# Scan output taken from the state, skip scaled ahead of the merge, one convolution tap moved, six score tiles instead of seven

## The chip, the cores and the metric

The kernel runs on one core of a Trainium2 chip. The metric is the device time of one execution in microseconds (us). TensorE (PE) does matmuls and transposes, VectorE (DVE) and ScalarE (ACT) do elementwise work, GpSimd (POOL) a little of it, and SyncE (SP) issues nearly all DMAs. All data are fp32.

## The reference

The input is (4, 64, 64, 256). A first layer, a Mamba-like block, is followed by self-attention over the 4096 positions of each image. Cut to what matters:

```
xz = layernorm(x) @ in_proj_W ;  x_proj, z = split(xz)              # 384 channels each
windows = 2x2 windows of x_proj                                     # 4 tokens each
# for each direction (forward, and backward on flipped windows):
dt = silu(dt_raw @ dt_W + dt_b);  dA = exp(dt * a);  dBx = dt * B * x    # 8 states n
state = dA_t * state + dBx_t ;  y_t = sum_n state[n] * C_t[n] ;  y += x * D
y_ssm = 0.5 * (y_fwd + y_bwd)
y_conv = gelu(depthwise3x3(x_proj) @ pw_W)
y = alpha * y_ssm + (1 - alpha) * y_conv ;  x_out = x + (y * silu(z)) @ out_W
x1 = x_out + mlp(layernorm(x_out))
# attention, per image:
scores = (x1 Wg + bg)(x1 Wf + bf)^T ;  out = gamma * (softmax(scores) (x1 Wh + bh) Wo + bo) + x1
```

## The kernel before

The layer is cut into 32 blocks of 8 image rows (`at` = 0 to 31, 8 blocks an image); a block is 512 positions, and its four window tokens t = 0 to 3 are four groups of 128 windows on the partitions. Each block runs `scan(at)` and, beside it, the generators of `side(at)`: the convolution of the block before (`conv`, `depthwise`), its gate, its `tail` (pointwise matmul, output projection, MLP, and the attention's inputs, written to DRAM) and the `head` of the next. Every `yield` gives a cost by which `first_layer` interleaves them. The instructions are recorded in that order; a scheduler then sets the order in which they stand on each engine.

In the scan, `decays` computes on ScalarE `e = exp(dt * a_n)` for one state and direction (L392). `turned` transposes 128x128 pieces of e on TensorE into a PSUM bank (L449; three banks, and a fourth in image 0). Then VectorE does, for each step j = 3n + k (state n, k = 0 to 2) and each direction d:

- `decayed`: p = dA * h, where h is the state so far (L461), or, for the first step, dA * B * u (L457), with u = dt * x;
- `given`: y[t] += p * C (L467);
- `carried`: h = u * B + p for k < 2 (L476).

y thus takes only the decayed part p. The part of u that enters at token t itself is put in once for all states: `cb` = sum over n of B * C, and y[t] starts as u0 * cb (ScalarE, L424) plus u1 * cb (VectorE, L426), for all four tokens. The forward direction is one step ahead of the backward one. The order of a step is p forward, p backward, y forward, h forward, h backward, y backward.

`merge` turns y back to channels (L554), adds the skip x * (D_f + D_b) on VectorE (L555, `dsum`), then scales by alpha / 2 on ScalarE (L558, `half_a`). `depthwise` sums nine taps: in image 0 two of three channel groups are done on TensorE wholly, in the other images only the first group, and of it seven taps on TensorE (L567) and two on VectorE (L584, L588).

Attention of image b starts when its 8 blocks are done. Narrow queries (`attend`, 128 positions) go in 8 steps; after each, `next(beside)` moves the next query's `weights` on by one stage, and `fill(RATE)` adds 7.2 us worth of the layer. `weights` computes scores transposed in two groups g of four PSUM banks q0 to q3 (L836), which the layer's matmuls use too (`aside`); ScalarE copies each pair of banks to one tile e of the pool `ep` (tag "eq", L844), so a query has four tiles, and step k of `attend` (L1030) reads tile k // 2:

```
for k in range(NI):                    # NI = 8
    ...
    nc.tensor.matmul(acc[:, : DIM + 1], lhsT=es[k // 2][:, k % 2, a : a + P], rhs=vt[:, s, :], ...)
    next(own, None)
    next(beside, None)
    fill(RATE)
```

Maxima (L850, L852), the subtraction (L871) and the exponential (L872) follow. With `EBUF = 7` the pool has seven such tiles. When the layer is finished, the rest of the queries go by twos (`late_weights`, `attend_late`, L929, L937, L1008), in buffers of other pools.

Of the kernel before, what the change touches and what calls it, by code (L numbers as in the profile page):

```python
# [21 lines left out]
F32 = mybir.dt.float32  # L22
AF = mybir.ActivationFunctionType
ALU = mybir.AluOpType
# [4 lines left out]
P = 128  # L29
DIM = 256  # L30
INNER = 384
NST = 8
RANK = 48
KD = DIM // P
KI = INNER // P
KF = 2 * DIM // P
VBUF = 5
EBUF = 7
ROWS = 8
TOK = 512  # L40
CK = DIM // 8
# [18 lines left out]
def block_then_attention_kernel(  # L60
# [18 lines left out]
    nc = tc.nc  # L79
# [26 lines left out]
    wp = ctx.enter_context(tc.tile_pool(name="w", bufs=1))  # L106
# [26 lines left out]
    vp = ctx.enter_context(tc.tile_pool(name="vp", bufs=VBUF))  # L133
    ep = ctx.enter_context(tc.tile_pool(name="ep", bufs=EBUF))
    ps = ctx.enter_context(tc.tile_pool(name="ps", bufs=3, space=PSUM))
# [8 lines left out]
    def bank():  # L144
        return ps.tile([P, TOK], F32, tag="ps", name="bank")
# [50 lines left out]
    dsum = wp.tile([P, KI], F32, name="dsum")  # L196
# [2 lines left out]
    nc.scalar.activation(alpha, v("gate", 0, KI), AF.Sigmoid)  # L199
    half_a = wp.tile([P, KI], F32, name="half_a")  # L200
    nc.vector.tensor_scalar(half_a, alpha, 0.5, None, ALU.mult)
    one_a = wp.tile([P, KI], F32, name="one_a")
    nc.vector.tensor_scalar(one_a, alpha, -1.0, 1.0, ALU.mult, ALU.add)
    b_fg = wp.tile([P, 1], F32, name="b_fg")
# [182 lines left out]
    def decays(at, n, d):  # L387
        _, _, dts, es = steps[at]
        e = three.tile([P, KI, 3 * P], F32, tag="e", name="e")
        lo = P * (1 - d)  # L390
        for f in range(KI):
            nc.scalar.activation(  # L392
                e[:, f, :], dts[d][:, f, lo : lo + 3 * P], AF.Exp,
                scale=a_sc[:, d, f * NST + n : f * NST + n + 1],
            )
        es[d, n] = e
# [16 lines left out]
    def scan(at, ensue):  # L413

        bc, cb, dts, es = steps[at]
        if at == 0:
            yield from inputs(at, 0)
        yield from inputs(at, 1)
        decays(at, 0, 1)
        u = us[at, 0], us[at, 1]  # L420
        y = one.tile([P, 4, INNER], F32, tag="y", name="y")

        for t in range(4):
            nc.scalar.activation(y[:, t, :], u[0][:, t, :], AF.Copy, scale=cb[:, 2 * t : 2 * t + 1])  # L424
        for t in range(4):
            nc.vector.scalar_tensor_tensor(  # L426
                y[:, t, :], u[1][:, t, :], cb[:, 2 * t + 1 : 2 * t + 2], y[:, t, :], ALU.mult, ALU.add
            )
            if t % 2:
                yield 1.1  # L430

        order = ((0, 1, 2, 3), (3, 2, 1, 0))
        hs = {}

        def place(d, j):

            if at < NBLK and (2 * j + d) % 4 == 3:
                return pso.tile([P, TOK], F32, tag="pso", name="pa")  # L440
            return bank()

        def turned(d, j):

            n, k = divmod(j, 3)
            off = (order[d][k + 1] - (1 - d)) * P
            pa = place(d, j)
            for f in range(KI):
                nc.tensor.transpose(pa[:, f * P : (f + 1) * P], es[d, n][:, f, off : off + P], ident)  # L449
            return pa  # L450

        def decayed(d, j, pa):
            n, k = divmod(j, 3)
            t0 = order[d][k]
            p = three.tile([P, INNER], F32, tag="p", name="p")
            if k == 0:
                nc.vector.scalar_tensor_tensor(  # L457
                    p, pa[:, :INNER], bc[:, t0, d, n : n + 1], u[d][:, t0, :], ALU.mult, ALU.mult
                )
            else:  # L460
                nc.vector.tensor_tensor(p, pa[:, :INNER], hs[d], ALU.mult)  # L461
            return p

        def given(d, j, p):
            n, k = divmod(j, 3)
            t = order[d][k + 1]
            nc.vector.scalar_tensor_tensor(  # L467
                y[:, t, :], p, bc[:, t, d, NST + n : NST + n + 1], y[:, t, :], ALU.mult, ALU.add
            )

        def carried(d, j, p):
            n, k = divmod(j, 3)
            if k < 2:
                t = order[d][k + 1]
                hs[d] = three.tile([P, INNER], F32, tag="h", name="h")
                nc.vector.scalar_tensor_tensor(  # L476
                    hs[d], u[d][:, t, :], bc[:, t, d, n : n + 1], p, ALU.mult, ALU.add
                )

        early = True  # L480
        pas = {}
        if early:
            pas[0, 0] = turned(0, 0)
        for j in range(3 * NST + 1):
            n, k = divmod(j, 3)
            first, second = j < 3 * NST, j > 0
            if early and k == 2 and n + 1 < NST:
                decays(at, n + 1, 1)
            if not early and first and k == 0 and n > 0:
                decays(at, n, 1)  # L490
            if first and k == 1 and n + 1 < NST:
                decays(at, n + 1, 0)
            if not early:
                if first:
                    pas[0, j] = turned(0, j)
                if second:
                    pas[1, j - 1] = turned(1, j - 1)
            p0 = decayed(0, j, pas.pop((0, j))) if first else None
            p1 = decayed(1, j - 1, pas.pop((1, j - 1))) if second else None
            if first:  # L500
                given(0, j, p0)
                if early:
                    if j + 1 < 3 * NST:
                        pas[0, j + 1] = turned(0, j + 1)
                    pas[1, j] = turned(1, j)
                yield 1.3
                carried(0, j, p0)
            if second:
                carried(1, j - 1, p1)
                given(1, j - 1, p1)  # L510
            yield 2.0
            if j == 3 * NST - 4:
                ensue = ensue()
            if j >= 3 * NST - 4:
                for cost in ensue:
                    yield cost
                    if j < 3 * NST and cost > 2.0:
                        break
        merged[at] = y
# [27 lines left out]
    def merge(at):  # L547

        y = merged.pop(at)
        xc = heads[at][1]  # L550
        for f in range(KI):
            py = bank()
            for t in range(4):
                nc.tensor.transpose(py[:, t * P : (t + 1) * P], y[:, t, f * P : (f + 1) * P], ident)  # L554
            nc.vector.scalar_tensor_tensor(xc[:, f, :], xc[:, f, :], dsum[:, f : f + 1], py, ALU.mult, ALU.add)  # L555
            yield 1.1
        for f in range(KI):
            nc.scalar.activation(xc[:, f, :], xc[:, f, :], AF.Copy, scale=half_a[:, f : f + 1])  # L558

    def depthwise(ydw, dense, taps):  # L560

        for f in range(KI):
            if f < dense:
                pc = aside()
                for tap in range(taps):
                    dy, dx = divmod(tap, 3)
                    nc.tensor.matmul(  # L567
                        pc, lhsT=diags[9 * f + tap], rhs=xp[:, f, dy : dy + ROWS, dx : dx + W],
                        start=(tap == 0), stop=(tap == taps - 1),
                    )  # L570
                    if tap % 3 == 2:
                        yield 2.6
                if taps == 9:
                    nc.scalar.copy(ydw[:, f, :], pc)
                    continue
            o = ydw[:, f, :].rearrange("p (r c) -> p r c", r=ROWS)
            for tap in range(taps if f < dense else 0, 9):
                dy, dx = divmod(tap, 3)
                x_tap = xp[:, f, dy : dy + ROWS, dx : dx + W]
                w_tap = v("dw", 9 * f + tap)  # L580
                if tap == 0:
                    nc.vector.tensor_scalar(o, x_tap, w_tap, None, ALU.mult)
                elif f < dense and tap == taps:
                    nc.vector.scalar_tensor_tensor(  # L584
                        o, x_tap, w_tap, pc.rearrange("p (r c) -> p r c", r=ROWS), ALU.mult, ALU.add
                    )
                else:
                    nc.vector.scalar_tensor_tensor(o, x_tap, w_tap, o, ALU.mult, ALU.add)  # L588
                if tap % 3 == 2:
                    yield 2.0  # L590
# [3 lines left out]
    def conv(at):  # L594
        b = at // NBLK
        ydw = one.tile([P, KI, TOK], F32, tag="ff", name="ydw")
        ydws[at] = ydw
        yield from depthwise(ydw, KI - 1 if b == 0 else 1, 9 if b == 0 else 7)

    def next_head(at):  # L600

# [460 lines left out]
    while True:  # L1062
        b, q = divmod(a, NQ)
# [119 lines left out]
```

## Time and profile before

| | |
|---|---|
| median of three runs | 5304.44 us (5290.6 to 5309.06) |
| profiled execution, its time | 5294.06 us |
| its span | 5292.2 us |
| TensorE matmul / weight load, busy | 4958.2 us (94%) / 3545.8 us (67%) |
| VectorE busy | 4574.8 us (86%), 8433 instructions |
| ScalarE busy | 3573.8 us (68%), 5499 instructions |
| granted TensorE clock, mean | 0.981 |

"Busy" is the time in which at least one instruction of an engine runs. The end of a matmul is modelled, so TensorE's busy time is an upper value. A row of the groups by line gives the source line, engine, operation, tiles written and read, shapes and count, then the busy time and the mean ns of one instruction, then the idle time of the engine just ahead of it and what ended that. A line of the stretches gives, for each engine, its busy us and in brackets its instructions.

### The profile page before, as it was taken

The numbers are of one execution on the slowest core, as the hardware profiler recorded it, in microseconds if no ns is written. First come the engines' busy times: TensorE is split into PE (matmuls) and PEld (weight loads), VectorE is DVE, ScalarE is ACT, GpSimd is POOL, SyncE is SP. The second block draws the span as 40 slices with busy tenths as digits, with TensorE's granted clock in tenths as the row PEclk, the third lists the DMA queues.
The fourth block names the chain that finished last, engine by engine and source line by source line (L and its number), as shares of the span: only waits on it lengthen the run. The fifth ranks groups of instructions, "written<-read, shape, count | busy, mean of one in ns | idle before, by whom it ended". The sixth has DMA issues, their size and how long they took to land. (4 is left out here: it accounts for less than half of the span.)

```text
span 5292.2 us, 77188 instructions
## 1 busy us (share of the span) xinstructions
PE 4958.2 (94%) x27186; PEld 3545.8 (67%) x27186; DVE 4574.8 (86%) x8433; ACT 3573.8 (68%) x5499; POOL 205.4 (4%) x304
## 2 busy tenths in 40 slices
PE   7999999999999999999999999999999999999999
PEld 4555565667666666666666666666667667888887
DVE  7999999999899888999999999988999976666665
ACT  5777777677767766777767777776677745555554
POOL 0000000000000000000000000000000000000000
PEclk7999999999999999999999999999999999999999
DMA  1001010334333333343333333433343335555554
GB/s 48 26 32 31 19 38 20 106 118 119 100 117 113 111 112 112 117 121 116 100 117 112 117 117 113 121 107 113 100 122 118 115 116 152 148 147 147 147 148 138
DMA packets 330291, 554.20 MB, mean 105 GB/s; under 512 B 51504, under 2 KB 85936, under 8 KB 329904
## 3 DMA queue, kind: packets, MB, share of 16 engines
q1 hardware_dynamic: 327328, 547.30, 35.2%
q8 instruction: 215, 3.52, 0.3%
q10 hardware_dynamic: 2576, 1.97, 0.1%
q14 instruction: 172, 1.41, 0.1%
HBM read 490.28 MB, written 58.79 MB: 104 GB/s over the span
## 5 line engine op out<-in xcount | busy, mean ns | idle before, releaser
L1030 PE MATMUL acc<-vt,eq 128*128 128x257 f32 x4736 | 1207.0, 391 | 25.3 <-DVE res L978 12.3
L392 ACT ACTIVATE e<-dt,a_sc 128x384 f32<-128x384 f32 x1536 | 851.9, 611 | 357.0 <-PE bank L449 350.3
L1030 PEld LDWEIGHTS acc<-vt,eq 128*128 128x128 f32 x4736 | 874.0, 194 | 256.2 <-issue 121.1
L467 DVE SCALAR_TENSOR_TENSOR y<-p,bc,y 128x384 f32<-128x384 f32 x1536 | 938.0, 611 | 0.4
L449 PEld LDWEIGHTS bank<-ident,e 128*128 128x128 f32 x4320 | 522.5, 143 | 323.9 <-issue 123.5
L449 PE MATMUL bank<-ident,e 128*128 128x128 f32 x4320 | 648.8, 280 | 81.1 <-DVE p L461 38.6
L1008 PE MATMUL bank<-vt,eT 128*128 128x257 f32 x2560 | 645.8, 382 | 0.0
L476 DVE SCALAR_TENSOR_TENSOR h<-u,bc,p 128x384 f32<-128x384 f32 x1024 | 613.0, 614 | 0.2
L461 DVE TENSOR_TENSOR p<-bank,h 128x384 f32<-128x384 f32 x960 | 512.6, 547 | 52.0 <-PE bank L449 50.9
L1008 PEld LDWEIGHTS bank<-vt,eT 128*128 128x128 f32 x2560 | 478.6, 189 | 83.7 <-issue 13.9
L844 ACT COPY eq<-q 128x512 f32<-128x512 f32 x592 | 302.6, 592 | 133.9 <-PE q L836 131.1
L942 DVE TENSOR_TENSOR mx<-mx,eT 128x512 f32<-128x512 f32 x378 | 261.7, 692 | 148.3 <-ACT eT L937 117.0
L872 ACT ACTIVATE eq<-eq 128x1024 f32<-128x1024 f32 x296 | 308.6, 1053 | 103.1 <-DVE eq L871 101.2
L871 DVE TENSOR_TENSOR eq<-eq,nb 128x1024 f32<-128x1024 f32 x296 | 358.6, 1223 | 7.6 <-ACT nb L867 6.8
L937 ACT COPY eT<-q 128x512 f32<-128x512 f32 x432 | 221.4, 597 | 198.7 <-PE q L929 198.7
L392 ACT ACT_TABLE_LOAD x256 | 328.4, 1283 | 40.1 <-PE bank L449 36.3
L852 DVE TENSOR_TENSOR mx<-mx,eq 128x512 f32<-128x512 f32 x444 | 308.8, 696 | 38.7 <-ACT eq L844 30.7
L588 DVE SCALAR_TENSOR_TENSOR ydw<-xp,vec,ydw 128x512 f32<-128x512 f32 x472 | 338.4, 743 | 1.2
L457 DVE SCALAR_TENSOR_TENSOR p<-bank,bc,u 128x384 f32<-128x384 f32 x480 | 291.6, 607 | 23.3 <-PE bank L449 23.0
L619 PE MATMUL q<-ydw,wpw 128*128 128x512 f32 x576 | 272.1, 603 | 16.8 <-ACT eq L844 16.6
L967 DVE TENSOR_TENSOR eT<-eT,m 128x1024 f32<-128x1024 f32 x216 | 247.6, 1219 | 42.3 <-ACT m L964 42.3
L1008 PE MATMUL acc<-vt,eT 128*128 128x257 f32 x896 | 273.9, 388 | 0.0
(152 smaller groups left out, 7282.1 us busy)
## 6 DMA issues: line engine op xcount, KB each, us to landing
vt<-vod SPq DMA_DIRECT2D x1616, 257.0 KB, 2.8
vod<-vst SPq DMA_DIRECT2D x32, 514.0 KB, 4.0
xo<-in_x_dram SPq DMA_DIRECT2D x256, 64.0 KB, 2.6
xt<-in_x_dram SPq DMA_DIRECT2D x256, 64.0 KB, 1.9
x1d<-xo SPq DMA_DIRECT2D x32, 512.0 KB, 2.9
res<-x1d SPq DMA_DIRECT2D x74, 128.0 KB, 2.7
out_dram<-res SPq DMA_DIRECT2D x296, 32.0 KB, 1.6
fgd<-fg SPq DMA_DIRECT2D x32, 256.0 KB, 2.0
```

The source lines that it names most:

```text
L392: nc.scalar.activation(e[:, f, :], dts[d][:, f, lo : lo + 3 * P], AF.Exp, scale=a_sc[:, d, f * NST + n : f * NST + n + 1],)
L449: nc.tensor.transpose(pa[:, f * P : (f + 1) * P], es[d, n][:, f, off : off + P], ident)
L461: nc.vector.tensor_tensor(p, pa[:, :INNER], hs[d], ALU.mult)
L467: nc.vector.scalar_tensor_tensor(y[:, t, :], p, bc[:, t, d, NST + n : NST + n + 1], y[:, t, :], ALU.mult, ALU.add)
L476: nc.vector.scalar_tensor_tensor(hs[d], u[d][:, t, :], bc[:, t, d, n : n + 1], p, ALU.mult, ALU.add)
L588: nc.vector.scalar_tensor_tensor(o, x_tap, w_tap, o, ALU.mult, ALU.add)
L844: nc.scalar.copy(e[:, j, :], pr[2 * a + j])
L852: nc.vector.tensor_tensor(mx, mx, e[:, r % 2, :], ALU.max)
L871: nc.vector.tensor_tensor(e8, e8, nb.unsqueeze(1).broadcast_to([P, 8, P]), ALU.add)
L872: nc.scalar.activation(e, e, AF.Exp)
L1008: nc.tensor.matmul(sums[c][:, : DIM + 1], lhsT=e[:, r % 2, s, c * P : (c + 1) * P], rhs=vt[:, s, :], start=(n == 0 and s == 0), stop=(n == ...
L1030: nc.tensor.matmul(acc[:, : DIM + 1], lhsT=es[k // 2][:, k % 2, a : a + P], rhs=vt[:, s, :], start=(n == 0 and s == 0), stop=(n == 2 * NI ...
```

## The change

- `given` reads h where `carried` forms one (k < 2) and p elsewhere. y[1] and y[2] then need no start from cb: the forward direction's first contribution (n = 0) starts them as a ScalarE copy with scale C. Only y[0] and y[3] start from u and cb.
- The order of a step is p forward, p backward, h forward, h backward, y forward, y backward. A dead switch (`early`) goes.
- `merge` scales the skip first on ScalarE, by `half_d` = alpha / 2 * (D_f + D_b), a new constant; VectorE then adds alpha / 2 times the turned y.
- In images 1 to 3 six taps of the first channel group are on TensorE and three on VectorE.
- `EBUF` is 6.

```diff
-EBUF = 7
+EBUF = 6
...
+    half_d = wp.tile([P, KI], F32, name="half_d")
+    nc.vector.tensor_tensor(half_d, half_a, dsum, ALU.mult)
...
-        for t in range(4):
+        for t in (0, 3):
             nc.scalar.activation(y[:, t, :], u[0][:, t, :], AF.Copy, scale=cb[:, 2 * t : 2 * t + 1])
-        for t in range(4):
+        for t in (0, 3):
             nc.vector.scalar_tensor_tensor(
                 y[:, t, :], u[1][:, t, :], cb[:, 2 * t + 1 : 2 * t + 2], y[:, t, :], ALU.mult, ALU.add
             )
-            if t % 2:
-                yield 1.1
+        yield 1.1
...
         def given(d, j, p):
             n, k = divmod(j, 3)
             t = order[d][k + 1]
-            nc.vector.scalar_tensor_tensor(
-                y[:, t, :], p, bc[:, t, d, NST + n : NST + n + 1], y[:, t, :], ALU.mult, ALU.add
-            )
+            h = hs[d] if k < 2 else p
+            c = bc[:, t, d, NST + n : NST + n + 1]
+            if d == 0 and n == 0 and k < 2:
+                nc.scalar.activation(y[:, t, :], h, AF.Copy, scale=c)
+            else:
+                nc.vector.scalar_tensor_tensor(y[:, t, :], h, c, y[:, t, :], ALU.mult, ALU.add)
...
             if first:
-                given(0, j, p0)
-                if early:
-                    if j + 1 < 3 * NST:
-                        pas[0, j + 1] = turned(0, j + 1)
-                    pas[1, j] = turned(1, j)
+                carried(0, j, p0)
+                if j + 1 < 3 * NST:
+                    pas[0, j + 1] = turned(0, j + 1)
+                pas[1, j] = turned(1, j)
                 yield 1.3
-                carried(0, j, p0)
             if second:
                 carried(1, j - 1, p1)
+            if first:
+                given(0, j, p0)
+            if second:
                 given(1, j - 1, p1)
             yield 2.0
...
-            nc.vector.scalar_tensor_tensor(xc[:, f, :], xc[:, f, :], dsum[:, f : f + 1], py, ALU.mult, ALU.add)
+            nc.scalar.activation(xc[:, f, :], xc[:, f, :], AF.Copy, scale=half_d[:, f : f + 1])
+            nc.vector.scalar_tensor_tensor(xc[:, f, :], py, half_a[:, f : f + 1], xc[:, f, :], ALU.mult, ALU.add)
             yield 1.1
-        for f in range(KI):
-            nc.scalar.activation(xc[:, f, :], xc[:, f, :], AF.Copy, scale=half_a[:, f : f + 1])
...
-        yield from depthwise(ydw, KI - 1 if b == 0 else 1, 9 if b == 0 else 7)
+        yield from depthwise(ydw, KI - 1 if b == 0 else 1, 9 if b == 0 else 6)
```

More of the change, by code (lines that the diff above doesn't have):

```diff
@@ L478, in carried @@
                 )
-        early = True
-        pas = {}
-        if early:
-            pas[0, 0] = turned(0, 0)
+        pas = {(0, 0): turned(0, 0)}
         for j in range(3 * NST + 1):
@@ L486, in scan @@
             first, second = j < 3 * NST, j > 0
-            if early and k == 2 and n + 1 < NST:
+            if k == 2 and n + 1 < NST:
                 decays(at, n + 1, 1)
-            if not early and first and k == 0 and n > 0:
-                decays(at, n, 1)
             if first and k == 1 and n + 1 < NST:
                 decays(at, n + 1, 0)
[L493 to L497, printed above, removed]
             p0 = decayed(0, j, pas.pop((0, j))) if first else None
@@ L500, in scan @@
             if first:
-                given(0, j, p0)
-                if early:
-                    if j + 1 < 3 * NST:
-                        pas[0, j + 1] = turned(0, j + 1)
-                    pas[1, j] = turned(1, j)
+                carried(0, j, p0)
+                if j + 1 < 3 * NST:
+                    pas[0, j + 1] = turned(0, j + 1)
+                pas[1, j] = turned(1, j)
                 yield 1.3
-                carried(0, j, p0)
             if second:
                 carried(1, j - 1, p1)
+            if first:
+                given(0, j, p0)
+            if second:
                 given(1, j - 1, p1)
```

## The prediction

> **What bounds the kernel now.** I read the stretches first (the page's 40 slices show where to cut: DMA jumps at 890 us, where attention begins beside the block layer, and VectorE drops at 4365 us, where the layer is done), then the groups by line, then the timeline of VectorE inside one block, then the waits.
>
> ```profile
> core 0: us, PE busy (x) PEld busy (x) DVE busy (x) ACT busy (x) POOL busy (x), PEclk, DMA share, GB/s
> 0.00:890.00 890.00, 812.41 (x3474) 503.01 (x3474) 837.24 (x1717) 643.26 (x1040) 54.60 (x87) 0.96 0.10 31
> 890.00:4365.00 3475.00, 3225.82 (x18356) 2293.61 (x18354) 3148.86 (x5876) 2474.14 (x3785) 150.79 (x217) 0.98 0.38 112
> 4365.00:5292.20 927.20, 919.96 (x5361) 749.14 (x5359) 588.72 (x841) 456.35 (x675) 0.00 (x0) 1.00 0.51 147
> ```
>
> Three stages. Stage 1, 890 us, 8 blocks (image 0) alone: VectorE 94%, and its first 57 us are start-up (24 us busy), so after that 812.75 of 833 us, 97.6%: VectorE is the bound. Stage 2, 3475 us, 24 blocks with 74 attention queries beside them: VectorE 3149 us (90.6%) and TensorE 3226 us (92.8%, with modelled ends) bound it together; ScalarE has 1001 us free. Stage 3, 927 us, wide queries: TensorE alone, 99%. The change touches the block layer and the queries of stage 2, so I cost stage 3 at nothing.
>
> ```profile
> L467 DVE SCALAR_TENSOR_TENSOR y<-p,bc,y 128x384 f32<-128x384 f32 x1536 | 938.0, 611 | 0.4
> L476 DVE SCALAR_TENSOR_TENSOR h<-u,bc,p 128x384 f32<-128x384 f32 x1024 | 613.0, 614 | 0.2
> L588 DVE SCALAR_TENSOR_TENSOR ydw<-xp,vec,ydw 128x512 f32<-128x512 f32 x472 | 338.4, 743 | 1.2
> L424 ACT ACTIVATE y<-u,cb 128x384 f32<-128x384 f32 x128 | 71.3, 617 | 3.8 <-issue 2.8 <-PE bank L554 0.8 <-ACT xp L531 0.2
> L426 DVE SCALAR_TENSOR_TENSOR y<-u,cb,y 128x384 f32<-128x384 f32 x128 | 71.0, 611 | 2.6 <-ACT u L409 1.6
> L558 ACT ACTIVATE xc<-xc,half_a 128x512 f32<-128x512 f32 x96 | 64.6, 718 | 20.7 <-DVE xc L555 20.5
> L844 ACT COPY eq<-q 128x512 f32<-128x512 f32 x592 | 302.6, 592 | 133.9 <-PE q L836 131.1 <-PE acc L1030 2.6
> ```
>
> See that the scan's own rows have almost no idle time ahead of them (0.4 and 0.2 us): VectorE hardly ever stands inside the scan, so an instruction less there is time less.
>
> ```profile
> 2501.99 3.08 DVE L852 TENSOR_TENSOR mx<-mx,eq 128x512 f32<-128x512 f32 x4 [1.11 <-ACT eq L844]
> ...
> 2508.21 1.14 DVE L476 SCALAR_TENSOR_TENSOR h<-u,bc,p 128x384 f32<-128x384 f32 x2
> ...
> 2523.25 1.28 DVE L405 TENSOR_TENSOR uT<-dt,xc 128x512 f32<-128x512 f32 x2
> ...
> 2527.50 2.73 DVE L588 SCALAR_TENSOR_TENSOR ydw<-xp,vec,ydw 128x512 f32<-128x512 f32 x4
> ```
>
> The timeline gives what one instruction really occupies: two h of 0.61 us end after 1.14, so one follows 0.53 us behind the other (the last 80 ns overlap); four taps of 0.74 us take 2.73, so 0.66 each. Instructions that read what the one just ahead wrote don't overlap: four mx take 3.08, 0.80 each, where two uT of the same size take 1.28, 0.60.
>
> **The change part by part**, with counts from the order in which both built programs' instructions stand.
>
> (1) Output from the state. h = u*b + p already holds what cb added for that state, so cb is needed for tokens 0 and 3 alone, and for n = 0, forward, the first two givens become a ScalarE copy that starts y. VectorE per block: 2 of L426 and 2 of L467 fall away, 128 in 32 blocks (8433 instructions become 8330 with the taps and half_d). ScalarE: 2 of L424 go, 2 copies of the same size come: zero. At 0.529 us: 4 x 0.529 = 2.12 us a block, 16.9 in stage 1, 50.8 in stage 2.
>
> (2) Taps. Blocks of images 1 to 3 (24): one tap from TensorE to VectorE: +24 x 0.663 = +15.9 us of VectorE; TensorE loses 24 x 2 passes of 512 columns. The wpw passes of this size last 603 ns and a row of them in the timeline follows at 0.43 us: -0.86 us a block, -20.6 in all. This one lies beside VectorE's work; it would be worth 20 us only where TensorE ends last. I count it at nothing, and as a reserve against added waits.
>
> (3) Order p, h, y. In the built order 82 more VectorE instructions of stage 2 read what the one straight ahead wrote, mostly y right behind its h or the other direction's y; 18 fewer do so with a separate wait ahead. The rows: mx with a separate wait costs 0.80 - 0.60 = 0.195 us; in the trace's start times, pairs without it begin 35 ns after the end instead of 80 ns before, 0.115 us. So +82 x 0.115 - 18 x 0.195 = +5.9 us in stage 2; no such pair is added in stage 1. Here a rule speaks otherwise: the Trainium skill, "VectorE: DVE Perf Modes", section "The DRAIN you can't avoid", says that the next operation can't start before the pipe is empty and that a semaphore between chained operations costs nothing extra. By that each removed instruction would free its whole 0.61 us and the new order would be free: -128 x 0.611 + 24 x 0.743 = -60 us. By the rows it is -16.9 - 50.8 + 15.9 + 5.9 = -46 us. I take the rows.
>
> (4) The ScalarE copy on VectorE's path. Per block the first copy has 10 or more VectorE instructions (5 us) between its h and the first reader; the second has 2 to 7, 1.06 us at the least and about 2 us in the middle. The copy takes 0.617 us and two handovers. Below nothing: excluded, since the saving is counted in (1). Above: ScalarE may be inside a 1.05 us exponential or a 1.28 us table load when h comes, some 1.5 us x 32 = 48 us. The row nearest is L426 waiting for ScalarE's u, 1.6 us in 128: small, so I take 0.2 us x 32 = 6 (2 in stage 1, 4 in stage 2). In front of the copy, ScalarE itself stands until h is there; behind it are exponentials for later states and score copies; its 1001 free us cover that.
>
> (5) Merge. Same counts. ScalarE's scaling no longer waits for VectorE (the 20.5 us of its idle time go), and VectorE's merge (L555, with the same duration) now waits for ScalarE instead: bounds -5 (x is ready earlier for the tail) and 96 x 0.5 = +48 us if ScalarE is late each time. The scaling depends on nothing recent, and the built order has it ahead; I take 0.
>
> (6) Six score tiles. A query holds four; of the next query's four, the third now takes the slot of the tile in use for steps 0 and 1, and the fourth that of steps 2 and 3. In the built order the fourth tile's slot is still to be read when its scores are done in 72 of 73 cases (7 with seven tiles), with a median of 13 PE instructions between, of which 8 passes L1030 take 1.9 us: the last two copies come 2 to 3 us later, and two of the four q banks that the layer shares stay full. The built order also moved other TensorE and ScalarE work into that gap; in 27 of 73 nothing stands between on ScalarE. Bounds: below, -30 us, since the layer's matmuls, which now wait for L844 (17 us of idle time ahead of L328 alone), come later in the order; above, 74 x 2.5 = +185 us. The row nearest is L844's present wait for scores, 131 us in all, whose cost ScalarE absorbs. I take 0.
>
> (7) Small: one yield of 1.1 less per block moves the interleaving; 74 narrow and 27 wide queries stay. ScalarE's table loads fall by 5 (6 us, under cover). Counts of DMAs on SP's queue, and POOL's order, are as before; the value loads land in 2.8 us and four are ahead.
>
> Sum: stage 1 -16.9 + 2 = -15; stage 2 -50.8 + 15.9 + 5.9 + 4 = -25, taken whole because TensorE sheds 21 us as well; together about -39. The profiled execution took 5294.06 us (span 5292.2): 5255. The median of the three runs, 5304.44, lies 10 us above it and the runs spread over 18, so I leave 5255.
>
> ```profile
> ACT e L392 <- PE bank L449: 350.3, 122, 8.5
> ACT eq L844 <- PE q L836: 131.1, 56, 10.2
> DVE p L461 <- PE bank L449: 50.9, 43, 4.7
> DVE mx L852 <- ACT eq L844: 30.7, 21, 5.5
> DVE mx L850 <- ACT eq L844: 26.7, 17, 3.6
> DVE p L457 <- PE bank L449: 23.0, 26, 3.7
> ```
>
> **The rivals.** These waits (total us, times, longest) are where they would show.
> - More than the sum: the new order lets TensorE pass the score copies, and part of its waits for L844 and of the 57 us that mx waits go. Half of some 90 us would give about 5210. For: the built order puts two or three groups of other matmuls ahead of the next use of a q bank. Against: VectorE stays at 90%.
> - Nothing: VectorE's saving in stage 2 turns into its waits for PE bank (51 and 23 us now) because TensorE is as full as VectorE; with (4) at its upper half, only stage 1's 15 us stay, less a few: about 5290 to 5300.
> - Slower: the sixth tile, (6). ScalarE stands in order before the third copy; exponentials for the decays behind it are late, so transposes, so p; and q banks stay full. It decides from 39/74 = 0.53 us a query; at 1.0 us, 74 us are lost and the time is 5330. For: 72 of 73. Against: ScalarE is ahead of TensorE already (350 us waiting for banks), so it has slack to lose.
>
> **How the numbers follow.** The sum 0.60 (its own range 5235 to 5275), more 0.14, nothing 0.13, slower 0.13. Some 0.3%, 16 us, is what can be told from no change: below 5288 is faster, above 5320 slower. Faster: 0.60 + 0.14 + a little of "nothing" = 0.76; same 0.11; slower 0.13. The range 5210 to 5318 leaves out about 0.07 below and 0.12 above.
>
> **What would show it.** Right: stage 1 some 875 us long with VectorE over 97% after start-up; stage 2 near 3450; stage 3 at 927; y rows at 0.61 us with less than 10 us waiting for the ScalarE copy; VectorE 45 to 50 us less busy. (4) wrong: the y row of the first backward given waits for ACT over 20 us. (5) wrong: the merge row waits for ACT. (6) wrong: a long wait of eq copies for acc of the attention matmuls, and q-bank rows waiting for the copies more than now. If stage 1 doesn't shorten by 10 us or more, the reading of VectorE as its bound is wrong.

## The result, and the profile after

The changed kernel takes 5264.57 us (median of 6 runs, 5262.73 to 5266.34), the kernel before 5300.45 us (median of 6): 36 us less, a ratio of 0.9933 with a 95% interval of 0.9920 to 0.9946. That is inside the range and near the forecast of 5255. The experiments show that it is so for the stated reason in stage 1, and mostly for another one in stage 2.

The stretches of the profile after, cut where attention starts and where the wide queries start (the same cuts in the profile before, at the first matmul of the scores and of the wide scores, lie at 888.6 and 4365.9 us):

```profile
core 0: us, PE busy (x) PEld busy (x) DVE busy (x) ACT busy (x) POOL busy (x), PEclk, DMA share, GB/s
0.00:876.10 876.10, 803.17 (x3443) 497.13 (x3443) 818.84 (x1679) 656.23 (x1048) 55.54 (x87) 0.97 0.10 31
876.10:4335.30 3459.20, 3220.08 (x18341) 2286.89 (x18340) 3117.57 (x5810) 2461.73 (x3769) 148.25 (x217) 0.98 0.37 113
4335.30:5260.90 925.60, 917.38 (x5357) 747.52 (x5356) 590.09 (x843) 459.01 (x678) 0.00 (x0) 1.00 0.49 146
```

Stage 1 is 12.5 us shorter, stage 2 18.1, stage 3 0.7: 31.3 in the profiled executions (span 5292.2 to 5260.9). Exactly cut, stage 2 of before had VectorE busy for 3150 of 3477.3 us, so idle for 327; now it is 342. The VectorE time that went there did not all come out of the stage.

The groups by line of the profile after (busy us, mean ns of one, then the idle time ahead and what ended it):

```profile
L480 DVE SCALAR_TENSOR_TENSOR h<-u,bc,p 128x384 f32<-128x384 f32 x1024 | 612.5, 612 | 0.4
L473 DVE SCALAR_TENSOR_TENSOR y<-h,bc,y 128x384 f32<-128x384 f32 x960 | 588.4, 613 | 3.7 <-ACT y L471 1.1
L473 DVE SCALAR_TENSOR_TENSOR y<-p,bc,y 128x384 f32<-128x384 f32 x512 | 312.4, 610 | 0.2
L428 DVE SCALAR_TENSOR_TENSOR y<-u,cb,y 128x384 f32<-128x384 f32 x64 | 36.9, 611 | 2.3 <-ACT u L411 1.1 <-ACT y L426 0.5
L583 DVE SCALAR_TENSOR_TENSOR ydw<-xp,vec,ydw 128x512 f32<-128x512 f32 x496 | 358.7, 742 | 1.6
L471 ACT ACTIVATE y<-h,bc 128x384 f32<-128x384 f32 x64 | 39.2, 612 | 27.1 <-DVE h L480 27.1
L552 DVE SCALAR_TENSOR_TENSOR xc<-bank,half_a,xc 128x512 f32<-128x512 f32 x96 | 66.9, 740 | 0.5 <-PE bank L550 0.4
L839 ACT COPY eq<-q 128x512 f32<-128x512 f32 x592 | 308.5, 587 | 193.8 <-PE q L831 114.0 <-PE acc L1025 79.0
```

The y rows are 1472 where they were 1536, and the y start 64 where it was 128: the 128 instructions are gone. VectorE waits 1.1 us in all for the new ScalarE copy (L471), which stands 27.1 us waiting for h. The merge (L552) does not wait for ScalarE. The last row carries the sixth tile: score copies now wait 79.0 us for attention's matmuls (acc), where it was 2.6.

The waits of the profile after (total us, times, longest):

```profile
ACT e L394 <- PE bank L450: 265.0, 107, 8.2
ACT eq L839 <- PE q L831: 114.0, 48, 7.8
ACT eq L839 <- PE acc L1025: 79.0, 40, 8.6
DVE xo L672 <- PE q L668: 65.7, 31, 11.4
DVE p L462 <- PE bank L450: 54.2, 33, 6.2
```

ScalarE's 79 us for acc came out of its wait for banks (350 before, 265 now): its slack paid, as the prediction had it. But VectorE's wait for TensorE in the MLP's second half (xo) grew to 65.7 us. Before, it was:

```profile
DVE xo L677 <- PE q L673: 44.3, 25, 7.9
```

In stage 2 it is VectorE that waits for TensorE more.

### The profile page after: what moved, and what is told of

It reads as the page before. It is cut to its first block, busy times and chain, and to the rows that moved or that the text cites. A ratio compares the mean times of both kernels' runs of the same rounds, so it can differ in the third digit from the quotient of the medians.

```text
span 5260.9 us, 76434 instructions
## 1 busy us (share of the span) xinstructions
PE 4940.6 (94%) x27138; PEld 3531.5 (67%) x27138; DVE 4526.5 (86%) x8330; ACT 3577.0 (68%) x5494; POOL 203.8 (4%) x304
## 5 line engine op out<-in xcount | busy, mean ns | idle before, releaser
L1025 PE MATMUL acc<-vt,eq 128*128 128x257 f32 x4736 | 1209.9, 390 | 20.6 <-issue 8.1
L473 DVE SCALAR_TENSOR_TENSOR y<-h,bc,y 128x384 f32<-128x384 f32 x960 | 588.4, 613 | 3.7 <-ACT y L471 1.1
L462 DVE TENSOR_TENSOR p<-bank,h 128x384 f32<-128x384 f32 x960 | 517.2, 548 | 55.4 <-PE bank L450 54.2
L839 ACT COPY eq<-q 128x512 f32<-128x512 f32 x592 | 308.5, 587 | 193.8 <-PE q L831 114.0
L866 DVE TENSOR_TENSOR eq<-eq,nb 128x1024 f32<-128x1024 f32 x296 | 358.9, 1222 | 12.5 <-ACT nb L862 12.3
L583 DVE SCALAR_TENSOR_TENSOR ydw<-xp,vec,ydw 128x512 f32<-128x512 f32 x496 | 358.7, 742 | 1.6
L473 DVE SCALAR_TENSOR_TENSOR y<-p,bc,y 128x384 f32<-128x384 f32 x512 | 312.4, 610 | 0.2
```

The costliest lines, as they stand in the source:

```text
L473: nc.vector.scalar_tensor_tensor(y[:, t, :], h, c, y[:, t, :], ALU.mult, ALU.add)
L839: nc.scalar.copy(e[:, j, :], pr[2 * a + j])
L866: nc.vector.tensor_tensor(e8, e8, nb.unsqueeze(1).broadcast_to([P, 8, P]), ALU.add)
```

## The experiments

Each was timed in five rounds against the kernel before on the same chip; the stage lengths are from its one profiled execution. "Changed" below is 5264.57 us, ratio 0.9933, stages 876.1 / 3459.2 / 925.6. It was timed only in the session of the result, where the kernel before took 5300.45 us; in the sessions of the experiments the kernel before took 5292 to 5295. So the distances by medians that follow are larger by up to 9 us when they are taken from the ratios. A profiled execution lies up to 10 us from the median of its kernel, so a few us between two stage lengths say nothing.

**Seven tiles.**

```diff
-EBUF = 6
+EBUF = 7
```

> The changed kernel with seven score tiles in place of six, nothing else. Theory (the sixth tile is absorbed: ScalarE's 79 us of waiting for acc comes out of slack): stage 1 as with six tiles, 876 us from start to first scores, and the total within 8 us of 5265; the wait of eq copies for acc goes from 79 us to under 5. Rival (the sixth tile costs what the sum of the prediction is short of, about 7 us in stage 2, or more): 10 to 40 us faster than 5265, all in stage 2.

5286.59 us, ratio 0.9975 (0.9965 to 0.9985): 22 us slower than the changed kernel, all in stage 2 (872.9 / 3483.1 / 928.5). Theory and rival are both wrong: going from seven tiles to six neither costs nothing nor costs time, it gains. The view of one source line gives what it waits for and who waits for it. The score copies (L839) in stage 2 of the changed kernel, with seven tiles, then with six:

```profile
  PE acc L1025: 7.8, 4
...
  PE q L614: 21.5, 19
  PE q L330: 21.0, 13
...
  PE q L668: 16.1, 13
```

```profile
  PE acc L1025: 79.0, 40
...
  PE q L330: 16.3, 11
  PE q L614: 13.1, 11
  PE q L668: 13.0, 10
```

The first line of each is ScalarE's own wait; the others are TensorE's, for q banks that the copies still hold. Added over all matmul rows of stage 2, TensorE waits 102.7 us for the score copies with seven tiles and 76.7 with six. The stage differs by 23.9. The traces also show how: between a group's last score and the next matmul into a q bank, TensorE has 14.6 other instructions in the mean with seven tiles and 20.6 with six (148 groups), so the copies have more time.

**Five tiles.**

```diff
-EBUF = 6
+EBUF = 5
```

> The changed kernel with five score tiles: of the next query's four tiles three have to wait for tiles in use. Theory (the wait for a tile is absorbed while ScalarE has slack; more of it is not): ScalarE's wait for acc grows from 79 us to 200 to 300, and the total rises by 10 to 60 us over 5265, all of it in stage 2. Rival (the wait is free at any depth, since scores are made a whole query ahead): within 8 us of 5265. A second rival (it costs 1 us a query already with six): 75 us or more above.

5300.8 us, ratio 1.0009 (1.0001 to 1.0017): 36 slower than the changed kernel, nearly all of it in stage 2 (874.3 / 3498.6 / 928.4), as the theory said. ScalarE waits 272 us for acc. TensorE's wait for score copies falls further, to 45 us, but its wait for the output's res, 6.7 with six tiles, is 36.2.

```profile
874.30:4372.90 3498.60, 3245.80 (x18342) 2295.09 (x18341) 3126.75 (x5808) 2443.44 (x3752) 152.89 (x217) 0.97 0.37 112
```

TensorE's idle time explains only 14 of the 39 us. With as many instructions as in the changed kernel it is busy for 26 us longer, at a lower granted clock; see the end of this part. Of the three sizes tried, six is the best.

**Seven taps and nine taps.**

```diff
-        yield from depthwise(ydw, KI - 1 if b == 0 else 1, 9 if b == 0 else 6)
+        yield from depthwise(ydw, KI - 1 if b == 0 else 1, 9 if b == 0 else 7)
```

(and 9 in place of 7 in the other)

> The changed kernel with seven taps on TensorE and two on VectorE in images 1 to 3, as before the change. VectorE is relieved of 24 x 0.66 = 16 us, TensorE gets 24 x 0.86 = 21 us. Theory of the prediction (VectorE ends last in stage 2, TensorE's part is hidden): 10 to 16 us faster than 5265. Rival (TensorE ends as often: the two offset each other): within 8 us of 5265. Second rival (TensorE ends last): 10 to 20 us slower. Stage 1 unchanged in all three.

> The changed kernel with all nine taps of the first channel group on TensorE in images 1 to 3: VectorE is relieved of 24 x 3 x 0.66 = 48 us less nothing, ScalarE gets 24 copies, TensorE 24 x 3 x 0.86 = 62 us. VectorE alone as the bound: 30 to 48 us faster than 5265. TensorE alone: 40 to 62 us slower. Both together: within 15 us either way.

Seven: 5271.22 us, 0.9952 (0.9940 to 0.9965), stages 872.9 / 3464.3 / 927.3; 7 us over the changed kernel by the medians, 10 by the ratios and 5 by stage 2. The intervals overlap, so this does not tell the two rivals apart; but it is not the 10 to 16 us less that VectorE as the bound requires. Nine: 5292.96 us, 0.9995 (0.9988 to 1.0001), 28 slower, stage 2 at 3482.5. VectorE is then busy for 38 us less and idle for 403 us of the stage, TensorE busy for 47 us more:

```profile
872.80:4355.30 3482.50, 3267.26 (x18487) 2309.40 (x18486) 3079.60 (x5738) 2449.70 (x3772) 153.63 (x217) 0.98 0.38 112
```

The time lies between what was expected of TensorE alone (40 to 62 us slower) and of both together. Half of TensorE's 47 us shows in the stage, and nothing of VectorE's 38: TensorE ends last more often.

**Eight more VectorE instructions a block**, of the same form and size as those taken away.

```diff
+            if d == 0 and k == 0:
+                nc.vector.scalar_tensor_tensor(y[:, 0, :], h, nil, y[:, 0, :], ALU.mult, ALU.add)
```

(nil is a column of zeros)

> The changed kernel with eight VectorE instructions more in each block (y[0] = 0 * h + y[0], forward, k = 0, same form and size as the ones that the change took away; the values stay as they are). At 0.529 us that is 4.2 us a block: 34 us in stage 1 and 102 us in stage 2. Theory (VectorE ends last in both stages): 90 to 100% of it shows in stage 1, and 70 to 100% in stage 2: stage 1 905 to 912 us long, total 5365 to 5400. Rival (in stage 2 TensorE ends as often and VectorE has 9% idle, so about half of it is hidden): stage 1 the same, stage 2 longer by 40 to 60, total 5335 to 5360. Counted at the 0.611 us of its row in place of 0.529: 39 and 117 us.

5348.89 us, 1.0107 (1.0092 to 1.0121). Stage 1 is 37.0 us longer (913.1), 0.58 us for each of 64: VectorE is its bound. From 57 us on it is busy for 31.3 us more, 0.49 for each, and idle for 5.7 more, for a wait of the layernorm came up (xt for rstd, 8.7 us where it was 1.2) that the run with one yield below has too, without any added work. Stage 2 is 45.5 us longer (3504.7), 0.24 for each of 192, in the rival's range. Its stretch, to set beside that of the changed kernel:

```profile
913.10:4417.80 3504.70, 3243.80 (x18348) 2300.15 (x18348) 3217.37 (x6001) 2460.70 (x3767) 150.66 (x217) 0.97 0.38 112
```

VectorE's idle time falls from 342 to 287 us: about half of the added work went into gaps. But 24 of the 45.5 us are TensorE's: with as many instructions it is busy for 3243.8 us where it was 3220.1, again at a lower clock.

**y started on VectorE.**

```diff
-                nc.scalar.activation(y[:, t, :], h, AF.Copy, scale=c)
+                nc.vector.tensor_scalar(y[:, t, :], h, c, None, ALU.mult)
```

> The changed kernel with the first two contributions to y formed on VectorE (one tensor-scalar multiplication of 128x384 each) in place of the ScalarE copy: 64 VectorE instructions more, of about 0.33 to 0.40 us each, worked out from the 256-wide one at 0.41 us long that follows at 0.33: 2 per block, 0.7 to 0.9 us a block. Theory (VectorE loses little by waiting for the copy): 18 to 25 us slower than 5265, of which 6 us in stage 1. Rival (in stage 1, where the second copy has only 1.06 us of other VectorE work beside it, VectorE waits as long as it saves): stage 1 within 2 us of 876, total within 10 us of 5265.

5272.19 us, 0.9962 (0.9950 to 0.9974), stages 882.7 / 3469.2 / 928.8: 8 us slower by the medians, 15 by the ratios. (Its profiled execution, 5282.65, is the slowest of five by 10 us.) Stage 1 has the 6 to 7 us that the theory asked for; the total lies between theory and rival. The ScalarE copy is the better place, and VectorE pays for it with 1.1 us of waiting.

**h and y of one direction, then of the other.**

```diff
                 carried(0, j, p0)
+                given(0, j, p0)
...
                 carried(1, j - 1, p1)
-            if first:
-                given(0, j, p0)
-            if second:
                 given(1, j - 1, p1)
```

> The changed kernel in the order p, p, then h and y of the forward direction, then h and y of the backward one: each y straight behind the h that it reads, where the record is kept by the scheduler. Theory (an instruction that reads what the one ahead wrote starts 0.115 us later): two such pairs in two of three steps, 32 pairs a block more at the most: up to 3.7 us a block, 29 us in stage 1 and 88 us in stage 2 if nothing stands between; half of it in stage 2, where other work stands between: total 5300 to 5360. Rival (chained instructions cost nothing extra): within 8 us of 5265.

5260.73 us, 0.9942 (0.9929 to 0.9954): not to be told from the changed kernel, stages 876.3 / 3450.8 / 927.2. This does not test the price of a chained pair: the scheduler pulls the pairs apart again, and in its trace 620 VectorE instructions start only behind the end of the one ahead whose output they read, where the changed kernel has 606. From the timeline of VectorE in stage 1 of this run:

```profile
343.39 0.61 DVE L458 SCALAR_TENSOR_TENSOR p<-bank,bc,u 128x384 f32<-128x384 f32 x1
343.92 0.61 DVE L473 SCALAR_TENSOR_TENSOR y<-h,bc,y 128x384 f32<-128x384 f32 x1
344.44 0.55 DVE L462 TENSOR_TENSOR p<-pa,h 128x384 f32<-128x384 f32 x1
344.91 0.61 DVE L480 SCALAR_TENSOR_TENSOR h<-u,bc,p 128x384 f32<-128x384 f32 x1
345.43 0.61 DVE L473 SCALAR_TENSOR_TENSOR y<-p,bc,y 128x384 f32<-128x384 f32 x1
345.96 0.61 DVE L473 SCALAR_TENSOR_TENSOR y<-h,bc,y 128x384 f32<-128x384 f32 x1
```

The forward h of 344.91 is read at 345.96, two later, though the source has them in sequence. (The p of 343.39 is the forward direction's first step, the p from pa is backward.)

**The output from the state alone** (with its order p, h, y and its single yield), on the kernel before: seven tiles, seven taps and the old merge.

```diff
 # the changed kernel, with
+EBUF = 7
+        yield from depthwise(ydw, KI - 1 if b == 0 else 1, 9 if b == 0 else 7)
+            nc.vector.scalar_tensor_tensor(xc[:, f, :], xc[:, f, :], dsum[:, f : f + 1], py, ALU.mult, ALU.add)
...
+            nc.scalar.activation(xc[:, f, :], xc[:, f, :], AF.Copy, scale=half_a[:, f : f + 1])
```

> The kernel before with the output from the state and the order p, h, y alone: seven tiles, seven taps, the merge as before. Theory (that part carries all of the gain, and the taps cost VectorE 16 us that they do not bring back): 5245 to 5258, faster than the whole change. Rival (the taps pay by relieving TensorE, and the merge by its shorter chain): 5265 to 5285, slower than the whole change.

5288.81 us, 0.9991 (0.9982 to 1.0000), stages 874.5 / 3487.1 / 925.4. The theory falls: stage 1 gains its 14 us, and stage 2 is 10 us longer than before, with 96 fewer VectorE instructions in it.

```profile
874.50:4361.60 3487.10, 3241.25 (x18392) 2297.51 (x18391) 3117.30 (x5787) 2465.43 (x3779) 147.95 (x217) 0.98 0.38 112
```

VectorE is busy for 33 us less than before and idle for 43 more (370 against 327). The next three runs ask where that went.

**Six tiles alone**, on the kernel before.

```diff
-EBUF = 7
+EBUF = 6
```

> The kernel before with six score tiles in place of seven, nothing else. The changed kernel lost 22 us of its 36 when it was given seven tiles back. Theory (six tiles help by themselves: the copies that wait make the scheduler put other TensorE work between the scores and the next use of a q bank): 5268 to 5282, stage 2 some 15 to 25 us shorter than 3477, stage 1 as before, 889. Rival (six tiles only help together with the new order of the scan, which leaves TensorE waiting for score copies longer): 5290 to 5305. The prediction's own fear (six tiles cost): over 5305.

5274.52 us, 0.9963 (0.9949 to 0.9976), stages 888.8 / 3457.5 / 926.3: the theory. One number brings 20 us, all in stage 2:

```profile
888.80:4346.30 3457.50, 3228.09 (x18394) 2292.61 (x18393) 3146.46 (x5879) 2440.19 (x3758) 150.41 (x217) 0.98 0.39 113
```

TensorE is as busy as before (3228.1 us in both) and idle for 229 us where it was 249: these 20 us are the stage's 20. Its waits for score copies fell by more than that, from 86.8 to 62.3, and the other TensorE instructions behind a group of scores rose from 13.8 to 18.3. The view of the copies' line (L844), before and with six tiles:

```profile
  PE acc L1030: 2.6, 1
...
  PE q L328: 17.0, 17
  PE q L619: 16.6, 15
```

```profile
  PE acc L1030: 52.0, 37
...
  PE q L328: 13.0, 15
  PE q L619: 9.6, 7
```

**One yield in place of two**, on the kernel before; no instruction differs.

```diff
-            if t % 2:
-                yield 1.1
+        yield 1.1
```

> The kernel before with one yield of 1.1 in place of two at the start of y, so that the layer is recorded against the attention steps a little differently; no instruction is added, taken away or changed. Theory (where the interleaving falls is worth 10 to 30 us in stage 2 by itself, either way, and that is where the 25 us went that the output from the state alone did not bring): stage 2 differs from 3477 by 10 us or more. Rival (pacing is neutral): stage 2 within 6 us of 3477 and the total within 8 us of before. Stage 1 the same within 1 us in both.

5316.47 us, 1.0048 (1.0035 to 1.0061), stages 901.4 / 3488.0 / 925.3. The theory holds for stage 2 (10.7 us longer), and stage 1, which both expected unchanged, is 12.8 longer. VectorE's waits in stage 1 from 57 us on, before and with one yield:

```profile
DVE h L275 <- POOL rstd L273: 8.5, 8, 1.2
...
DVE xt L275 <- POOL rstd L273: 1.0, 1, 1.0
```

```profile
DVE h L275 <- POOL rstd L273: 9.7, 8, 1.2
DVE xt L275 <- POOL rstd L273: 8.7, 7, 1.2
```

The layernorm goes from VectorE to GpSimd and back. In the kernel before, the scheduler had other VectorE work in that gap; now seven of eight blocks stand there for about 1.2 us. These waits are 8.9 of the 12.8 us; VectorE is also busy for 4.0 us longer with the same 1637 instructions, which they do not explain. In stage 2 the wait that grew is the one that also grew in the changed kernel, xo, 44.3 before:

```profile
DVE xo L676 <- PE q L672: 75.9, 34, 11.4
```

**The order p, h, y alone**, on the kernel before, y still from p, both yields kept.

```diff
-                given(0, j, p0)
+                carried(0, j, p0)
...
-                carried(0, j, p0)
             if second:
                 carried(1, j - 1, p1)
+            if first:
+                given(0, j, p0)
+            if second:
                 given(1, j - 1, p1)
```

> The kernel before with the order p, p, h, h, y, y of a step alone: y still takes p, and starts from cb for all four tokens, with both yields. VectorE's work is the same. Theory (the new order, in which the transposes of the next step no longer stand behind y, costs stage 2 its 25 us with seven tiles): 15 to 35 us slower than before, in stage 2. Rival (the order is neutral, and the ScalarE copies or the pacing cost it): within 8 us of before.

5300.63 us, 1.0012 (1.0003 to 1.0020), stages 902.1 / 3474.5 / 924.8. Stage 2 is 2.8 us shorter: the rival, as far as stage 2 goes. Stage 1 is 13.5 longer, again with xt waiting for rstd (9.9 us), which neither had expected.

**Four taps.**

```diff
-        yield from depthwise(ydw, KI - 1 if b == 0 else 1, 9 if b == 0 else 6)
+        yield from depthwise(ydw, KI - 1 if b == 0 else 1, 9 if b == 0 else 4)
```

> The changed kernel with four taps of the first channel group on TensorE and five on VectorE in images 1 to 3. From the runs with more VectorE work (102 us more, stage 2 longer by 45, so 0.45 each) and with nine taps (48 us less on VectorE, 62 more on TensorE, stage 2 longer by 23, so 0.72 for TensorE): two taps more on VectorE are +31.8 x 0.45 = +14, two less on TensorE -41.3 x 0.72 = -30, together -15: about 5249, faster than the changed kernel. Rival (VectorE, at 90%, takes over as the bound): 5265 to 5285. Stage 1 unchanged.

5279.97 us, 0.9974 (0.9963 to 0.9984), stages 873.8 / 3481.5 / 927.6: 15 slower than the changed kernel, where the slopes gave 15 faster.

```profile
873.80:4355.30 3481.50, 3192.32 (x18245) 2274.20 (x18244) 3144.61 (x5858) 2469.54 (x3779) 149.58 (x217) 0.97 0.38 112
```

TensorE is busy for 28 us less, not 41, and idle for 50 more; its transposes wait 85 us for p (56 in the changed kernel). So six taps lie between two losses, and slopes from one side did not carry to the other. In the kernels with four and nine taps the yields of the convolution fall elsewhere too (for this channel group their costs add to 6.6 and 7.8 a block, with six or seven taps to 7.2); what that does was not tested apart, and the run with one yield shows that it can matter. No version in these runs is clearly faster than the changed kernel.

**What the granted clock adds.** The traces record the clock that TensorE is granted: it is either full or half. Stage 2 in the profiled executions, in us:

| | length | TensorE busy | TensorE idle | at half clock |
|---|---|---|---|---|
| before | 3477.3 | 3228.1 | 249.2 | 126 |
| before, six tiles | 3457.5 | 3228.1 | 229.4 | 126 |
| before, one yield | 3488.0 | 3229.0 | 259.0 | 109 |
| state alone | 3487.1 | 3241.3 | 245.8 | 143 |
| changed | 3459.2 | 3220.1 | 239.1 | 137 |
| changed, seven tiles | 3483.1 | 3222.3 | 260.8 | 140 |
| changed, five tiles | 3498.6 | 3245.8 | 252.8 | 188 |
| changed, eight more | 3504.7 | 3243.8 | 260.9 | 181 |
| changed, four taps | 3481.5 | 3192.3 | 289.2 | 191 |

Seven tiles against six is free of this, in both kernels: nearly the whole difference is idle time of TensorE. In the last three rows a part of the loss is the clock. It is no accident of one execution: the mean clock over the span is 0.980 to 0.981 in all six executions of the changed kernel, 0.977 to 0.979 in 13 with five tiles, 0.973 to 0.976 in 4 with eight more and 0.976 to 0.977 in 8 with four taps. The half-clock stretches follow waits. They begin on a grid of 3.41 us. In stage 2 of the changed kernel TensorE was busy for under 45% of 22 slices of this grid, and 20 of them are followed by half clock; of the 878 slices with over 80%, one is. With five tiles there are 31 such slices under 45%, 28 of them followed by half clock. So a wait that leaves a slice half empty mostly brings half clock, and many short waits do not. No run here sets the clock by itself, so how much of each loss is the clock's stays open.

## Why the prediction was right

**Stage 1: right, for its reason.** -15 was forecast, -12.5 measured. VectorE's busy time fell by 17.0 us (835.8 to 818.8) where 16.9 were forecast, 0.53 for each of 32 instructions; its idle time grew by 4.5, not by the 2 allowed for the copy. The largest new wait is uT's for a bank (7.1 us, 9 times). There is luck in it: one yield alone, or the new order alone, makes stage 1 some 13 us longer than before, mostly by waits of the layernorm that the changed kernel does not have (its xt waits 1.2 us). The prediction put the yield under "small" and had no reason to expect that.

**Stage 2: near in size, wrong in cause.** The sum had -50.8 + 15.9 + 5.9 + 4 = -25; measured was -18.1. (With stage 1 it gives -40, not the -39 that was subtracted.) Four steps of it fail:

- "at 0.529 us ... 50.8 in stage 2", taken whole. VectorE's busy time did fall as counted (32.7 us with the tap, 34.9 forecast). But against the kernel with the same single yield (3488.0), the output from the state, with its order, gives 3487.1: 0.9 us for 96 instructions. The 90.6% of VectorE was read as a bound beside TensorE's 92.8%, and "VectorE hardly ever stands inside the scan" was read from the rows of y and h alone. The scan's p rows do wait, 75 us in all, for TensorE's transposes (their rows stand below this list). Of the two executions compared, the one with the output from the state has VectorE idle for 33 us more, and TensorE idle for 13 us less but busy for 12 us longer, with more time at half clock. More work for VectorE does show (8 more a block), though half of that comes with a slower TensorE.
- (2), the tap: +15.9 us for VectorE and, for TensorE's part, "I count it at nothing". With seven taps in the changed kernel stage 2 is no shorter (5 us longer, which is within the scatter). So TensorE's part was worth about what VectorE's cost, or more.
- (6), six tiles, "I take 0". They carry stage 2: 23.9 us in the changed kernel, 19.8 in the kernel before. The mechanism written down under its lower bound (-30) is the one that showed: the layer's matmuls into q banks come later, behind other TensorE work (13.8 instructions became 18.3 in the kernel before), and TensorE waits less for the copies.
- (7), the yield, "small". Alone it costs the kernel before 12.8 us in stage 1 and 10.7 in stage 2.

The rows of p in the kernel before:

```profile
L461 DVE TENSOR_TENSOR p<-bank,h 128x384 f32<-128x384 f32 x960 | 512.6, 547 | 52.0 <-PE bank L449 50.9
L457 DVE SCALAR_TENSOR_TENSOR p<-bank,bc,u 128x384 f32<-128x384 f32 x480 | 291.6, 607 | 23.3 <-PE bank L449 23.0
```

In profiled stage-2 times the change goes thus: one yield +10.7; the output from the state, with its order and ScalarE copies, -0.9; merge and tap together -4.0; six tiles -23.9; sum -18.1. The merge was not run apart from the tap. Each figure holds in that sequence, and the two small ones are not told from nothing.

That the sum came out is luck: the saving on VectorE and the yield, counted at -50.8 and nothing, are missing from one side, and the six tiles, counted at nothing, make up for it on the other.

**(4), (5) and stage 3: right.** The copy costs VectorE 1.1 us (6 taken), the merge waits 0.5, stage 3 moved by 0.7. **(3)** is half open. The pairs were there: in stage 2 of the traces 182 instructions start 35 ns after the end of the one straight ahead whose output they read, where it was 99, so 83 more (82 forecast). But no run isolated their 5.9 us. The choice of the rows over the rule of the Trainium skill ("VectorE: DVE Perf Modes", "The DRAIN you can't avoid") is confirmed: in stage 1 each instruction freed 0.53 us of busy time, not 0.61. The section itself adds that "A next op that is not held starts earlier", which the prediction left out. And a separate wait is not free in such a pair: in the profile before, 385 of them start 104 ns after the end, 157 without it 35 ns after.

**The rivals.** "More than the sum" named the right wait (L844), but laid it to the new order, which alone moved stage 2 by 2.8 us; it is the six tiles that shorten this wait. "Nothing" named the right loser (VectorE's saving against a full TensorE), though against before its wait in xo grew (44.3 to 65.7 us) and that in p hardly did (50.9 to 54.2). "Slower" by the sixth tile is refuted at six; five tiles do cost, in part by the clock.

## What to carry to other kernels

Where two engines are both over 90% busy, test the slope before pricing an instruction: adding eight instructions a block, taking the output from the state alone and moving taps showed that an instruction added to VectorE and one removed from it are not worth the same. Read such a test with the other engine's busy time and clock beside it, or a slower TensorE passes for a longer VectorE. Where a scheduler sets the order, a pool size or a yield that changes no arithmetic can move as much as the arithmetic; change it alone before crediting a bundle to its most visible part. A buffer fewer is not always a wait more: it can move a wait to an engine that has slack.

## What the runs showed of the hardware that was not expected

A wait of TensorE can be paid for twice. With the same count of TensorE instructions in stage 2, its busy time was 3220 us in the changed kernel and 3246 with five tiles; the clock stood at half for 137 and 188 us, mostly (24 of 30 and 34 of 42 times) behind 3.41 us in which TensorE had been busy for less than half.

One price is worth keeping: a VectorE instruction of 128x384 that lasts 0.61 us took 0.58 us of a VectorE-bound stage (0.49 of it busy time) and 0.24 us of a stage in which TensorE ends last more often.
